# A two-layer graph network on one core: ten rounds of gathers placed between the set-up's tables, and the blocks' pieces dealt out singly

## The chip, the core and the metric

The kernel runs on one core of a Trainium2 chip. The engines named below are PE (matrix multiply; its weight loads are shown apart as PEld), DVE (vector), ACT (scalar), POOL, and SP, which here only issues transfers. The metric is the device time of one execution in microseconds (us), the median of the runs. Lower is better.

## The reference

Two rounds of mean aggregation over 200,000 directed edges between 12,500 nodes of 256 features, a third matrix product, a residual and a layer norm:

```python
def _sage_conv(x, src, dst, W_l, b_l, W_r):
    msgs = x[src]
    agg = jax.ops.segment_sum(msgs, dst, num_segments=N_NODES)
    deg = jax.ops.segment_sum(jnp.ones((src.shape[0],), x.dtype), dst, num_segments=N_NODES)
    mean = agg / jnp.maximum(deg, 1.0)[:, None]
    return mean @ W_l + b_l + x @ W_r
h = jax.nn.relu(_sage_conv(x, src, dst, W1_l, b1, W1_r))
h = jax.nn.relu(_sage_conv(h, src, dst, W2_l, b2, W2_r))
out = layernorm(x + (h @ W3 + b3))
```

Edges come sorted by `dst`, and `dst` is drawn as the square of a uniform number: nodes with a low number have many edges, the others few.

## The kernel before

**Blocks, hot and cold.** The 12,500 nodes are 98 blocks of 128 rows (`NB`). The first ten blocks in layer 1 (fourteen in layer 2) are hot. They are handled as a dense product: `count` builds a matrix of how often each source occurs for 256 targets, `product` (L605 to L614) multiplies it with all of `x`, held as three bf16 parts that add up to float32. The parts of `x` are made by `split_rows` (98 calls, each: load a block into `x_sb`, two casts on ACT and two subtractions on DVE in `exact`, store of `parts`); those of `h` are made in `first_block`.

**Rounds.** The edges of cold blocks go in rounds. A round is four gathers of 128 rows each from DRAM into one of four buffers `got` (L532, POOL), a 0/1 table `one` (L466, DVE), and four matmuls into `part_ps` (L543, PE). When a group of edges is complete (one or two rounds) `part_ps` is copied to `some` (L549, ACT), a round later `summed` multiplies it with a second 0/1 table `two` (L555; L560 for the in-degrees) and DVE adds the product to a ring of sums (`sums` L567, `degs` L563). Layer 1 has 269 rounds, that is 1,076 gathers; layer 2 has 247 rounds and 988 gathers. Layer 2 gathers rows of `h_d`, which layer 1 has just written, so its first gather waits for the last store of layer 1.

**Blocks in pieces.** When a block's sums are complete, its rows run through the weights: `first_block` in three pieces, `last_block` in five, each piece ending in a `yield`. `first_block`'s second piece multiplies the degree row with a one (L860) into column `ps[:, NC, 0:1]` of a PSUM tile, DVE reads it there (`deg`, L862, then the reciprocal L863), and then PE transposes the block's rows `x_sb` into the same tile (L814), which ACT copies to `own_t` (L816). `sage` (L837, L839, DVE L842 and L843, ACT L845) makes the layer's rows.

**What sets the order.** PE and POOL run in the order in which the program is written (`manual_schedule`), so a wait of one PE instruction holds up all behind it. The order on DVE, ACT and SP is chosen by a planner at build time, and each of them then also works strictly through its own list. `layer` writes the order of each layer: per round first `gathered(i)`; then half of the pieces that are due, where a quarter of all pieces of the up to three open blocks (`MOST`) counts as due; half of the dense work that is due (`fill`, by a table of costs); then `summed` of the round before; then the other half of pieces and of dense work. The first open block always goes first.

**Buffers that matter here.** `x_sb` is one pool of three buffers, used by `split_rows` and by the blocks alike (L803 to L811). `exact` has one buffer `rest` (L587), also used by both. `own` has one buffer.

**Set-up.** Before the layers, a set-up turns the edge lists into tables (L175 to L402): transposes on PE, many small operations on DVE. Its SBUF is given up at its end, and the two matrices `counts` (cleared by ACT at L430) lie in that space. PE and POOL follow the planner's order in the set-up, and the manual order only begins with `layer`.

Of the kernel before, what the change touches and what calls it, by code (L numbers as in the profile page):

```python
# [47 lines left out]
def by_runs(  # L48
# [123 lines left out]

    with tc.tile_pool(name="setup", bufs=1) as su, \
# [140 lines left out]


# [19 lines left out]
        for g, (c0, c1) in enumerate(spans):  # L335
            n = c1 - c0
            for begins, to, name in ((start, key_t[g], "key"), (nxt_first, after_t[g], "aft")):
# [12 lines left out]
            nc.vector.tensor_copy(offs[g], off_f[:, lows[g]:highs[g]])  # L350


# [7 lines left out]
                                       op1=OP.mult, accum_out=test())  # L360
        scr2 = su.tile([P, len(groups)], F32, name="scr2")
# [73 lines left out]
    part_pool = ctx.enter_context(tc.tile_pool(name="part_ps", bufs=1, space=PSUM))  # L435
    sum_pool = ctx.enter_context(tc.tile_pool(name="sum_ps", bufs=1, space=PSUM))
# [4 lines left out]
    REGS = 8  # L441

    class Values:


        def __init__(self, row, i0, engine, top):
            self.row, self.i0, self.engine, self.top, self.have = row, i0, engine, top, {}

        def at(self, i):
            if i not in self.have:  # L450
                a = i - self.i0
                n = min(REGS, self.row.shape[1] - a)
                _, v = nc.values_load_multi_w_load_instructions(
                    self.row[0:1, a:a + n], engines=[self.engine], min_val=0, max_val=self.top,
                    skip_runtime_bounds_check_because="it is clamped where it is made")
                self.have = {i + k: v[k] for k in range(n)}
            return self.have[i]


    def select(g, r, second):  # L460

        t0, n = groups[g]
        lo, c0 = (lo_t2, C2) if second and t0 // P == C2 else (lo_t, C0)
        a = t0 - c0 * P + r
        one = chosen_pool.tile([P, G, W], F32, name="one", bufs=AHEAD + 1)
        nc.vector.tensor_tensor(  # L466
            one, lo[:, a:a + n * (G - 1) + 1:n].unsqueeze(2).to_broadcast([P, G, W]),
            lane_b[:, :W].unsqueeze(1).to_broadcast([P, G, W]), op=OP.is_equal)
        if r < n - 1:
            return one, None  # L470
        two = chosen_pool.tile([P, P], F32, name="two", bufs=AHEAD + 2)
        nc.vector.tensor_scalar(two, lane_b, lo2[:, g:g + 1], None, op0=OP.is_equal)
        return one, two

    def left_after(g):

        return NB if g == len(groups) - 1 else min(max(int(at_least(groups[g + 1][0]) // P), 0), NB)

    AHEAD = 2

    MOST = 3

    def layer(table, hot, block, n_pieces, dense, dense_cost):
# [3 lines left out]

        def advance(i):
            b, p, left = queue[i]
            next(p)  # L490
            queue[i] = b, p, left - 1
            if left == 1:
                done.add(b)
                del queue[i]
                return True

        def begin():
            while waiting and len(queue) < MOST:
                b, *of = waiting.pop(0)
                queue.append((b, block(b, *of), n_pieces))  # L500
                advance(len(queue) - 1)

        def pieces(n):

            i = 0
            for _ in range(min(n, len(queue))):
                if not advance(i):
                    i += 1
            begin()
# [12 lines left out]
        begun = hot // P  # L522
        at = Values(place, 0, DVE, RN - 1)
        chosen = {i: select(*rounds[i], second) for i in range(AHEAD)}

        def gathered(i):

            (gr, r), g = rounds[i], got[i % NGOT]
# [764 lines left out]
```

## Time and profile before

| | |
|---|---|
| time, three runs | 2920.19, 2927.65, 2936.41 us; median 2927.65 us |
| the profiled execution | 3466.66 us, its span 3464.9 us |
| mean granted PE clock in it | 0.868 |
| PE busy in the span | 2583.9 us (75%), 18,630 matmuls |
| POOL busy | 2029.7 us (59%), nearly all gathers |
| DVE busy | 1468.1 us (42%) |
| ACT busy | 1250.0 us (36%) |
| DMA | 676.45 MB, mean 195 GB/s |

The profiled execution took 18% longer than the median of the runs. Sums over the profile are therefore made against 3464.9 us first and carried over to 2927.65 us in a second step. A group's row gives line, engine, operation, output and inputs, count, then busy time in us and the mean of one in ns, then the idle time of the engine just before these instructions and what ended it. A row of waits gives the engine and line that waited, what it waited for, the total in us, the number of times and the longest. In a timeline each row begins with the start and the duration in us, and ends in brackets with the idle time before it and what ended that.

The stages lie so in the span: set-up up to 74 us, layer 1 up to 1888 us, layer 2 behind it, last gather at 3404 us.

### The profile page before, as it was taken

The numbers are of one execution on the slowest core, as the hardware profiler recorded it, in microseconds if no ns is written. First come the engines' busy times: TensorE is split into PE (matmuls) and PEld (weight loads), VectorE is DVE, ScalarE is ACT, GpSimd is POOL, SyncE is SP. The second block draws the span as 40 slices with busy tenths as digits, with TensorE's granted clock in tenths as the row PEclk, the third lists the DMA queues.
The fourth block names the chain that finished last, engine by engine and source line by source line (L and its number), as shares of the span: only waits on it lengthen the run. The fifth ranks groups of instructions, "written<-read, shape, count | busy, mean of one in ns | idle before, by whom it ended". The sixth has DMA issues, their size and how long they took to land.

```text
span 3464.9 us, 54167 instructions
## 1 busy us (share of the span) xinstructions
PE 2583.9 (75%) x18630; PEld 1705.5 (49%) x18630; DVE 1468.1 (42%) x4350; ACT 1250.0 (36%) x2702; POOL 2029.7 (59%) x2074
## 2 busy tenths in 40 slices
PE   2544658778878878888886677777878887878885
PEld 1121225545545556656654354444555555656664
DVE  7656655444444444445453023333223233333433
ACT  1323655455554555556553013333111111111222
POOL 3554656665665565666663666666666666566661
PEclk9666679879979989989998888888889899999998
DMA  4544577648648648656753565666777787766762
GB/s 89 153 147 147 183 210 229 195 128 279 202 144 269 202 144 263 207 159 194 222 162 111 184 204 184 187 186 192 243 240 246 243 258 240 230 211 215 223 213 69
DMA packets 408134, 676.45 MB, mean 195 GB/s; under 512 B 59659, under 2 KB 266537, under 8 KB 407849
## 3 DMA queue, kind: packets, MB, share of 16 engines
q1 hardware_dynamic: 303415, 400.51, 36.8%
q0 software_dynamic: 99072, 270.66, 25.8%
q10 hardware_dynamic: 5362, 1.72, 0.3%
q8 instruction: 149, 2.44, 0.3%
q14 instruction: 136, 1.11, 0.1%
HBM read 582.80 MB, written 89.87 MB: 194 GB/s over the span
## 4 chain that ended last, share of the span: by engine, by line
PE 60%; issue 8%; another core or an unknown queue 8%; DVE 4%; DMA 3%; ACT 3%; SPq 0%; POOL 0%; ACTq 0%; DVEq 0%
PE dense_ps L614 22%; PE part_ps L543 8%; PE block_ps L837 6%; PE count_ps L682 6%; PE block_ps L839 5%; PE sum_ps L555 4%; PE block_ps L814 3%; PE block_ps L895 3%; ACT counts L688 1%; PE sum_ps L560 1%; DMA rows<-x_d 1%; DMA rows<-h_d 1%; PE count_ps L686 1%; DVE pick L637 1%
## 5 line engine op out<-in xcount | busy, mean ns | idle before, releaser
L532 POOL DMA_INDIRECT got<-in_x_dram,src_t x1076 | 1083.2, 1007 | 764.9 <-PE part_ps L543 282.7
L532 POOL DMA_INDIRECT got<-h_d,src_t x988 | 944.4, 956 | 610.1 <-issue 247.9
L614 PE MATMUL dense_ps<-counts,rows 128*128 128x256 bf16 x7056 | 1025.9, 289 | 84.3 <-issue 49.3
L688 ACT CAST counts<-count_ps 128x392 f32 (+2 forms) x1052 | 716.1, 681 | 633.2 <-PE count_ps L686 145.9
L614 PEld LDWEIGHTS <-rows 128*128 128x128 bf16 x7056 | 702.3, 103 | 338.0 <-issue 142.4
L543 PE MATMUL part_ps<-got,one 128*32 128x257 f32 (+1 forms) x4128 | 384.9, 438 | 96.2 <-issue 47.1
L682 PE MATMUL count_ps<-pick,low 128*128 128x392 bf16 (+2 forms) x1052 | 371.1, 381 | 104.8 <-DVE pick L637 33.3
L637 DVE TENSOR_SCALAR pick<-steps,key_t 128x686 bf16<-128x686 f16 (+2 forms) x748 | 300.0, 411 | 254.1 <-PE count_ps L682 77.3
L466 DVE TENSOR_TENSOR one<-lo_t,lane_b 128x128 f32<-128x128 bf16 x516 | 148.0, 287 | 539.6 <-PE part_ps L543 143.6
L549 ACT COPY some<-part_ps 128x257 f32<-128x257 f32 (+1 forms) x361 | 136.8, 379 | 562.0 <-remote 215.5
L567 DVE TENSOR_TENSOR sums<-sums,sum_ps 128x256 f32 x361 | 148.3, 411 | 303.2 <-remote 119.7
L555 PE MATMUL sum_ps<-two,some 128*128 128x128 f32 x1444 | 246.6, 297 | 5.4 <-remote 2.8
L555 PEld LDWEIGHTS sum_ps<-two,some 128*128 128x128 f32 x1444 | 212.6, 208 | 23.5 <-issue 8.5
L543 PEld LDWEIGHTS part_ps<-got,one 128*32 128x32 f32 x4128 | 89.9, 114 | 245.9 <-issue 178.0
L814 PE MATMUL block_ps<-ident,x_sb 128*128 128x128 f32 x196 | 50.7, 348 | 207.2 <-DVE deg L862 96.7
L842 DVE TENSOR_TENSOR own<-block_ps,biases 128x256 f32<-128x256 f32 x196 | 83.0, 423 | 259.8 <-PE block_ps L839 123.2
L682 PEld LDWEIGHTS <-low 128*128 128x128 bf16 x1052 | 108.3, 106 | 155.7 <-issue 72.1
L816 ACT COPY own_t<-block_ps 128x256 f32<-128x256 f32 x294 | 109.1, 374 | 188.7 <-PE block_ps L814 76.0
L563 DVE TENSOR_TENSOR degs<-degs,sum_ps 1x128 f32 x186 | 51.0, 274 | 232.0 <-PE part_ps L543 67.7
L895 PE MATMUL block_ps<-w_sb,own_t 128*128 128x256 f32 x392 | 122.1, 440 | 36.4 <-ACT own_t L816 25.3
L837 PE MATMUL block_ps<-w2l_sb,sums 128*128 128x256 f32 x336 | 112.6, 464 | 46.3 <-DVE sums L567 18.8
L641 DVE TENSOR_TENSOR low<-low_t,lane_b 128x512 bf16<-128x512 bf16 x187 | 128.1, 685 | 43.1 <-PE count_ps L686 28.1
(177 smaller groups left out, 2672.1 us busy)
## 6 DMA issues: line engine op xcount, KB each, us to landing
rows<-h_d SPq DMA_DIRECT2D x343, 384.0 KB
rows<-x_d SPq DMA_DIRECT2D x245, 384.0 KB
x_sb<-in_x_dram SPq DMA_DIRECT2D x291, 128.0 KB
count_d<-counts SPq DMA_DIRECT2D x28, 896.0 KB
counts<-count_d SPq DMA_DIRECT2D x28, 896.0 KB
x_d<-parts SPq DMA_DIRECT2D x98, 192.0 KB
h_d<-parts SPq DMA_DIRECT2D x98, 192.0 KB
got<-in_x_dram,src_t POOLq DMA_INDIRECT x1076
```

The lines of the kernel that those rows point to most:

```text
L532: nc.gpsimd.indirect_dma_start(out=g[:, j, :D], out_offset=None, in_=table, in_offset=bass.IndirectOffsetOnAxis(ap=src_t[:, e:e + 1], axis=0))
L543: nc.tensor.matmul(part_ps[j * W:(j + 1) * W, :width], lhsT=one[:, j], rhs=g[:, j, :width], start=r == 0, stop=r == n - 1)
L555: nc.tensor.matmul(sum_ps[:, c], lhsT=some[:, c * P:(c + 1) * P], rhs=two, start=True, stop=True)
L567: nc.vector.tensor_add(own, own, sum_ps[:, :NC])
L614: nc.tensor.matmul(ps[:, c], lhsT=rows[:, b % 2, k, c * P:(c + 1) * P], rhs=c_sb[:, b, :DN], start=False, stop=b == NB - 1 and k == 2 and ...
L637: nc.vector.tensor_scalar(r[:, :w * NB], steps[:, :w * NB], key_t[g][:, t - lo_g:t - lo_g + 1], None, op0=OP.is_equal)
L682: nc.tensor.matmul(ps[:, :(b - a) * NB], lhsT=s, rhs=r[:, a * NB:b * NB], start=True, stop=alone)
L688: nc.scalar.copy(to[:, :, bass.ds(n0 + a, b - a)], ps[:, :(b - a) * NB].rearrange("p (d s) -> p s d", s=NB))
L814: nc.tensor.transpose(ps[:, c], t[:, c * P:(c + 1) * P], ident)
L837: nc.tensor.matmul(ps[:, 0], lhsT=agg[:, c], rhs=wl[:, c], start=c == 0, stop=c == NC - 1)
L839: nc.tensor.matmul(ps[:, 1], lhsT=own_t[:, c], rhs=wr[:, c], start=c == 0, stop=c == NC - 1)
L895: nc.tensor.matmul(y[:, 0], lhsT=h2_t[:, c], rhs=w3_sb[:, c], start=c == 0, stop=c == NC - 1)
```

## The change

It has two parts. **Rounds in the set-up:** the state of the rounds moves into a class `Gathers` with a method `step`, which writes one round and returns the group that is ready to be summed. The first ten rounds of layer 1, with their matmuls and sums, are written into the set-up: one ahead of the tables for the hot blocks, one behind each of the seven pairs of tables, and two later. The manual order of PE and POOL begins there, so the set-up's remaining transposes stand in it too. `layer` starts at round ten. **Pieces:** each round has three turns. A turn advances one block by one piece at most, a block no sooner than two turns after its last piece (`APART`), and at most two blocks are open (`MOST`). Each turn is followed by a third of the dense work, and `summed` stands ahead of the third turn. With it, buffers and waits change: `split_rows` has its own buffers (`split_sb`, two), the blocks' `x_sb` has two, `exact` writes the rest over its input (or over `own`) and not into `rest`; the degree is copied by ACT together with the transposed rows and read by DVE from SBUF; `last_block` loads `x_sb` in its third piece instead of its first and adds the bias in the fourth instead of the third.

```diff
+    class Gathers:
+        def __init__(self, table, second):
...
+            self.chosen = {i: select(*self.rounds[i], second) for i in range(AHEAD)}
+            self.i, self.last = 0, None
+
+        def step(self):
+            before = self.last
+            self.last = self.gathered(self.i) if self.i < len(self.rounds) else None
+            self.i += 1
+            return before
...
         nc.vector.memset(zeros_b, 0.0)
+        ctx.enter_context(tc.manual_schedule(engines={PE, POOL}))
+        gathers_1 = Gathers(x, False)
+
+        def early_round():
+            before = gathers_1.step()
+            if before:
+                gathers_1.summed(*before, set())
+
+        early_round()
...
             nc.vector.tensor_copy(offs[g], off_f[:, lows[g]:highs[g]])
-
+            early_round()
+
+        early_round()
 
         nxt_f = su.tile([P, CH, P], F32, name="nxt_f")
...
         nc.vector.scalar_tensor_tensor(scr[:, C0:], rel[:, C0:], float(W), nxt_f[:, C0:], op0=OP.is_ge,
                                        op1=OP.mult, accum_out=test())
+        early_round()
...
-    MOST = 3
+    MOST, APART = 2, 2
...
         def begin():
-            while waiting and len(queue) < MOST:
+            if waiting and len(queue) < MOST:
                 b, *of = waiting.pop(0)
-                queue.append((b, block(b, *of), n_pieces))
-                advance(len(queue) - 1)
+                p = block(b, *of)
+                next(p)
+                queue.append([b, p, n_pieces - 1, turn + APART])
-        def pieces(n):
-            i = 0
-            for _ in range(min(n, len(queue))):
-                if not advance(i):
-                    i += 1
+        def pieces():
+            nonlocal turn
+            turn += 1
+            q = next((q for q in queue if q[3] <= turn), None)
+            if q:
+                next(q[1])
+                q[2:] = q[2] - 1, turn + APART
+                if q[2] == 0:
+                    done.add(q[0])
+                    queue.remove(q)
             begin()
...
-            n = -(-sum(left for _, _, left in queue) // 4)
-            pieces(-(-n // 2))
-            due = dense_cost * min(1.0, (i + 1) / (len(rounds) - 8))
-            fill(spent + (due - spent) * 0.5)
...
-            pieces(n // 2)
-            fill(due)
+            before = gathers.step()
+            due = dense_cost * min(1.0, (i + 1 - i0) / (n - i0 - 8))
+            for part in range(3):
+                if part == 2 and before:
+                    gathers.summed(*before, done)
+                    while begun < left_after(before[0]):
+                        waiting.append((begun,))
+                        begun += 1
+                pieces()
+                fill(spent + (due - spent) / (3 - part))
...
-    def exact(t, s):
-        rest = work.tile([P, D], F32, name="rest", bufs=1)
+    def exact(t, s, rest):
...
     def split_rows(b):
-        t = load_rows(x, N, b, "x_sb")
+        t = load_rows(x, N, b, "split_sb")
         s = work.tile([P, 3, D], BF16, name="parts")
-        exact(t, s)
+        exact(t, s, t)
...
-        t = work.tile([P, D], F32, name=name, bufs=MOST if table is x else 2)
+        t = work.tile([P, D], F32, name=name)
...
-    def transposed(t, ps, name):
+    def transposed(t, ps, name, more=0):
...
-        s = work.tile([P, NC, P], F32, name=name)
-        nc.scalar.copy(s, ps[:, :NC])
-        return s
+        s = work.tile([P, NC * P + 1], F32, name=name)
+        n = NC * P + more
+        nc.scalar.copy(s[:, :n], ps.rearrange("p c l -> p (c l)")[:, :n])
+        return s[:, :NC * P].rearrange("p (c l) -> p c l", l=P), s[:, NC * P:]
...
             nc.tensor.matmul(ps[:, NC, 0:1], lhsT=deg_row, rhs=ones[0:1, 0:1], start=True, stop=True)
-            deg = work.tile([P, 1], F32, name="deg")
-            nc.vector.tensor_scalar(deg, ps[:, NC, 0:1], 1.0, None, op0=OP.max)
+        x_t, deg = transposed(x_sb, ps, "own_t", int(of_ring))
+        if of_ring:
+            nc.vector.tensor_scalar(deg, deg, 1.0, None, op0=OP.max)
             nc.vector.reciprocal(rdeg[:, b:b + 1], deg)
-        x_t = transposed(x_sb, ps, "own_t")
         yield True
...
-        exact(h, s)
+        exact(h, s, own)
...
         h_sb = load_rows(h_d, NB * P, b, "h_sb")
-        x_sb = load_rows(x, N, b, "x_sb")
...
         if of_ring:
             nc.scalar.copy(agg, zeros)
+        x_sb = load_rows(x, N, b, "x_sb")
+        yield True
+        h2_t, _ = transposed(h2, turned(), "own_t")
         nc.vector.tensor_add(x_sb, x_sb, biases[:, 2])
-        yield True
-        h2_t = transposed(h2, turned(), "own_t")
         yield True
...
-    with tc.manual_schedule(engines={PE, POOL}):
-        layer(x, HG1 * DN, first_block, 3, staged(stages_1), cost_of(stages_1))
-        layer(h_d, HG * DN, last_block, 5, staged(stages_2), cost_of(stages_2))
+    layer(gathers_1, first_block, 3, staged(stages_1), cost_of(stages_1))
+    layer(Gathers(h_d, True), last_block, 5, staged(stages_2), cost_of(stages_2))
```

## The prediction

> **What bounds the kernel now.** I read the totals first, then the chain that ended last, then the waits of PE and POOL, then the same by stages, and last the timeline where the waits are longest. From the page, the chain and the gathers:
>
> ```profile
> PE 60%; issue 8%; another core or an unknown queue 8%; DVE 4%; DMA 3%; ACT 3%; SPq 0%; POOL 0%; ACTq 0%; DVEq 0%
> ...
> L532 POOL DMA_INDIRECT got<-in_x_dram,src_t x1076 | 1083.2, 1007 | 764.9 <-PE part_ps L543 282.7
> L532 POOL DMA_INDIRECT got<-h_d,src_t x988 | 944.4, 956 | 610.1 <-issue 247.9
> ```
>
> The chain is PE's: POOL has no share. The second thing to see is how near POOL is all the same. Between two gathers POOL always loses some 0.31 us ("issue": 508.5 us in 1,652 waits, next fence), so a gather costs 1.007 + 0.308 us in layer 1 and 0.956 + 0.308 in layer 2: 1,076 x 1.315 + 988 x 1.264 = 2,664 us. With the 27 us before the first gather, 38 us between the layers and 60 us after the last gather, POOL alone needs **2,789 us**, 139 less than the median of 2927.65. The profiled execution is 537 us longer than the median, and the chain gives 8% to "issue" and 8% to an unknown queue, together about as much. My reading: much of those two is the recording's own, and without it PE is quicker and POOL sets the pace wherever it isn't stopped. The profile can't prove that.
>
> The waits of PE, then of POOL:
>
> ```profile
> PE block_ps L814 <- DVE deg L862: 96.7, 70, 3.9
> PE block_ps L814 <- DMA x_sb<-in_x_dram: 78.0, 7, 15.2
> PE block_ps L814 <- ACT h L845: 58.9, 31, 5.5
> ...
> PE block_ps L895 <- ACT own_t L816: 25.3, 17, 4.6
> ...
> PE block_ps L814 <- DVE rest L594: 19.4, 2, 17.9
> ```
> ```profile
> POOL got L532 <- issue: 508.5, 1652, 1.1
> POOL got L532 <- PE part_ps L543: 371.1, 133, 24.7
> ```
>
> Four of PE's waits belong to the blocks' pieces and one to the split. Two kinds must be kept apart: waits of about 1 to 2 us (deg, h, own_t), which POOL rides out with four buffers, and waits of 15 us, in which POOL stops too. The stages show where (start:end, length, then busy us of PE, PEld, DVE, ACT, POOL, granted clock, DMA share, GB/s):
>
> ```profile
> 27.00:75.00 48.00, 14.20 (x54) 8.46 (x54) 44.44 (x162) 2.90 (x4) 19.26 (x16) 1.00 0.21 61
> 75.00:97.00 22.00, 6.43 (x28) 1.51 (x28) 10.84 (x30) 21.78 (x4) 8.26 (x8) 0.71 0.20 54
> 97.00:200.00 103.00, 61.69 (x300) 21.97 (x297) 75.50 (x210) 22.14 (x59) 64.88 (x63) 0.70 0.55 167
> 200.00:400.00 200.00, 95.27 (x513) 42.66 (x511) 126.46 (x329) 79.39 (x182) 107.23 (x105) 0.67 0.51 156
> 800.00:1000.00 200.00, 163.18 (x1281) 111.67 (x1278) 87.14 (x253) 109.82 (x222) 122.35 (x126) 0.89 0.69 214
> ```
>
> From 97 to 400 neither PE nor POOL is full. In the timeline of layer 1, one such stop and the end of the set-up:
>
> ```profile
> 218.75 0.66 PE L814 MATMUL block_ps<-ident,x_sb 128*128 128x128 f32 x2 [14.63 <-DMA x_sb<-in_x_dram]
> 222.53 0.95 POOL L532 DMA_INDIRECT got<-in_x_dram,src_t  x1 [10.37 <-PE part_ps L543]
> ```
> ```profile
> 74.20 22.01 ACT L430 COPY counts<-zero 128x13034 f32<-128x13034 f32 x2 [44.22 <-DVE scr L400]
> 75.78 1.34 POOL L532 DMA_INDIRECT got<-in_x_dram,src_t  x1 [24.73 <-PE part_ps L543]
> ```
>
> While PE waited, DVE and ACT did nothing but split rows: the block's load had its turn in the shared `x_sb` pool behind some six splits at 2.4 us each.
>
> **The change, part by part**, in us of the profiled execution.
>
> *Rounds in the set-up.* POOL stood 24.7 us for the set-up's end (row above) and 12.1 us more up to 98.3, because `some` was queued on ACT behind the 22 us of clearing. Ten rounds are 40 gathers. Beside the busy DVE of the set-up the first 16 took 19.22 us, 1.20 each, so 40 x (1.20 + 0.30) = 60: the last ends at 87, its strip is multiplied about 1.9 later (after the fourth gather of layer 2, which ended at 1893.35, the strip began at 1895.23). [...] The row decides: 1.20 in the set-up against 0.95 at 1888 to 1913 with DVE idle, the worst one 2.52; so I pay 0.25 each, no more.
> The order costs something. On PE the tables of pair g now stand behind strip g, at 27.2 + 6.0(g+1) + 1.9: the last pair goes at 71 and not at 58. DVE's own additions are ten `one` at 0.287 and four or five sets of `two`, `degs`, `sums` (0.97): 7 us. Its tests (59.2 to 74.0, 15 us) either fill the waits or follow. The set-up ends at 81 to 88; take 85, so clearing ends at 107, 11 later. By then POOL has issued 40 and four more rounds, 56 gathers, against 31 at that time now: 25 x 1.31 = 33 ahead. The count work starts 11 later, and DVE, 73% busy from 97 to 200, has to make it up. **-25**; between -37 (both stops gone, no price) and +11 (the delay alone).
>
> *Own buffers for the split and for blocks.* PE's 78.0 + 19.4 = 97.4; POOL's part_ps waits between 98.3 and 600 sum to 98.8. The new load waits only for a block two before. What is late next is POOL: between 97 and 500 it has 229 gathers at 1.037 + 0.308 = 308 of 403 us, so at most 95; DVE, with about 260, is close behind. **-90**, between -95 and -50 (the splits' stores and `parts`, still two buffers shared with blocks, could hold a block). `rest` and `own`, in place: nothing, hidden by the two turns to the same block's next piece; uncovered, a chain of five operations of 0.4 us per block.
>
> *The degree through ACT.* 70 waits, 96.7 us, go: nothing on DVE stands any more between L860 and the transposes. What replaces it is one column more in a copy of 0.37 us, and L862 and L863 with two turns before L843 needs them. L860's own wait for `degs` stays (31.6). PE alone waits here, 45 of them from 600 to 1600 where PE is 82% busy and POOL 61%. **-48** if PE paces, 0 if POOL does; -97 at best.
>
> *Singly dealt pieces.* Counting turns by the code, a block of layer 2 now waits half a round between two of its pieces (the first open block is often taken in both halves); two turns are two thirds of a round, 4 us at 6.2 us a round, against a chain L842, L843, L845 of 0.42 + 0.48 + 0.42 and its queues. Of 58.9 + 25.3 = 84 I take half. The later `x_sb` load in layer 2 has two turns, 4 us, for a landing of 2.7 (issued 3402.65, read at 3405.35) and for whatever SP waits for ahead of it: price +10. **-32** if PE paces, 0 if POOL does; bounds -84 and +80. Two open blocks are enough: layer 2's last blocks come at half a block a round, 2 of 3 turns. By the same count one block less is open behind the last round: **-3**.
>
> *The clock.* [...] 0.67 to 0.70 against 0.89, eight matmuls of a strip 1.08 against 0.64; [...] PE doesn't end that stage, so I count nothing.
>
> **The forecast, POOL's pace.** Then only the stops of POOL come back: -25 - 90 - 3 = -118, and 2927.65 - 118 = **2,810**, 21 above POOL's own 2,789. These stops (24.7 + 12.1 + 98.8 = 136) are also just what separates the median from 2,789, which is my reason for this case. Chance 0.42, own range 2,785 to 2,850.
>
> **Rivals.** (1) *PE's pace*, as the chain of the profile says: -25 - 90 - 48 - 32 - 3 = -198 of 3464.9, 5.7%, so 2,760. For it: the chain; against it: POOL's sum, unless a gather is quicker unrecorded. 0.22. (2) *The block waits all the same*, now for `parts` or for SP: half of the 90 and of the 25 goes, 2,870. For it: SP's and ACT's strict lists; against: the loads come a round early. 0.16. (3) *Slower: DVE stopped in front of the bias.* L889 stands in DVE's list, and its load in SP's behind loads of `rows`, which wait 3.1 us on average for PE to free a buffer in layer 2 (322.0 us in 105 waits) and 10.9 at worst. While DVE waits, `one`, `sums` and picks wait, then PE, then POOL. 98 blocks x 2 us = 196, less 118: 3,005; it decides from 1.2 us a block. For it: L889 waits 28.7 us now; against: it has a piece's matmuls and 4 us ahead of it. 0.13. (4) *No difference*: the stops belong to the recording. Against: 15 us is six splits, not a hiccup. 0.07.
>
> A change within 0.5% (2,913 to 2,942) can't be told from none. Faster 0.42 + 0.22 + 0.16 = 0.80, same 0.07, slower 0.13. The range goes from 2,715 (PE's pace with both costs nearer their best) to 2,930.
>
> **What would show it.** Right: no wait of PE for `x_sb` or `rest` beyond a few us; L862 gone from PE's waits; some 40 gathers issued by 90 us; DVE and POOL fuller from 97 to 400, clock above 0.8. Wrong: clearing of `counts` starting after 95; L889 waiting more than 100 us in all; deg's wait gone and the time down by 150 or more (rival 1).

## The result and the profile after

The changed kernel takes **2906.97 us** (median of 6 runs, 2895.08 to 2912.04) and the kernel before 2935.14 us (6 runs) beside it: ratio **0.9909**, 95% interval 0.9882 to 0.9935. The forecast was 118 us less than before; 28 us came.

The profiled execution of the kernel before that the prediction was made from (3466.66 us) is like those of one chip among the five used later, where this kernel takes 3472.27 us (median of 11 runs). On the other four it takes about 2,930, as in the runs above. So ratios are only formed with runs of the kernel before on the same chip, and below "before" is a new recording on a chip of the common kind (label b1_before_again, span 2936.8 us).

From the page of the changed kernel: the engines' busy time, the chain that ended last, and the two groups of gathers (busy us, mean ns, then the idle time ahead of them).

```profile
PE 2394.6 (82%) x18630; PEld 1632.6 (56%) x18630; DVE 1471.2 (51%) x4350; ACT 1253.6 (43%) x2702; POOL 2065.3 (71%) x2074
...
PE 54%; DMA 19%; POOL 8%; issue 7%; DVE 6%; ACT 4%; DVEq 0%; SPq 0%; ACTq 0%; POOLq 0%
...
L243 POOL DMA_INDIRECT got<-in_x_dram,src_t x1076 | 1116.7, 1038 | 446.5 <-issue 274.2
L243 POOL DMA_INDIRECT got<-h_d,src_t x988 | 946.4, 958 | 343.1 <-issue 285.3
```

The work is the same, PE still has the largest share of the chain, and a gather of layer 1 has become dearer (1.038 us; 1.010 in the new recording of before). The unknown queue is gone from the chain, as it is in b1 (whose chain accounts for 85% of its span): only the recordings of the slower chip show it.

The change's path shows best in where POOL stands. The table gives the start in us of the n-th gather, counted in the timelines of five kernels (columns 4 to 6 are experiments of the next section; the chips differ, but on each the kernel before takes about 2,930 us).

| gather | before | changed | parts apart (b4) | split spread (e3) | no split (d4) |
|---|---|---|---|---|---|
| 56 | 140.5 | 108.8 | 109.0 | 108.5 | 105.5 |
| 240 | 430.2 | 370.6 | 378.7 | 376.3 | 358.1 |
| 280 | 497.3 | 441.5 | 433.0 | 431.4 | 413.3 |
| 400 | 654.5 | 641.2 | 607.2 | 597.7 | 573.2 |
| 1076, last of layer 1 | 1567.8 | 1564.9 | 1523.6 | 1512.5 | 1488.3 |
| 2064, last of layer 2 | 2882.2 | 2854.6 | 2818.7 | 2793.0 | 2773.0 |

The changed kernel is 32 us ahead at gather 56, as forecast, and 60 at gather 240. Then it loses 46 of these in the next 160 gathers, and at the end of layer 1 it leads by 3. The 25 us that are left of the gain come from layer 2.

Two things eat the lead. Call it a stop when POOL idles for more than 0.5 us between two gathers, and count of it what goes beyond the usual 0.31. Then from gather 56 to the end of layer 1 the changed kernel has 95 us of stops and the kernel before 89, and its gathers are busy for 1,049 us and not 1,026. So of the 29 us of lead that go, 23 go in longer gathers and 6 in stops. The stops were to become fewer and only moved: between gathers 56 and 240 they fell from 41 to 5 us, between 240 and 400 they rose from 13 to 55.

What stops POOL is seen in the waits of PE and of POOL from 100 to 640 us (line that waited, releaser: total, times, longest). Before:

```profile
PE block_ps L814 <- DMA x_sb<-in_x_dram: 58.1, 6, 16.2
PE count_ps L682 <- DVE pick L637: 29.2, 20, 12.0
PE block_ps L814 <- DVE rest L594: 18.0, 1, 18.0
...
POOL got L532 <- PE part_ps L543: 57.0, 16, 11.5
```

The changed kernel, same stretch:

```profile
PE block_ps L886 <- DVE own L869: 54.3, 7, 19.1
PE count_ps L706 <- DVE pick L661: 23.8, 20, 3.7
...
POOL got L243 <- PE part_ps L254: 57.5, 16, 17.9
```

The wait for `x_sb` is gone, and so is the one for `rest`. In their place stands a wait that did not exist: the product of the degree row (L886) waits for a PSUM buffer that DVE's L869 is late to read. For POOL the sum has not changed: 57.0 us in 16 waits, 57.5 in 16. The timeline of the changed kernel at the longest stop (start, duration, in brackets the idle time before and its end) shows who is late:

```profile
456.15 0.40 ACT L617 CAST parts<-split_sb 128x256 bf16<-128x256 f32 x1 [6.15 <-DMA split_sb<-in_x_dram]
...
456.58 0.43 DVE L618 TENSOR_TENSOR split_sb<-split_sb,parts 128x256 f32<-128x256 f32 x1 [5.91 <-ACT parts L617]
...
457.93 1.61 SPq L626 DMA_DIRECT2D x_d<-parts  x1
458.27 0.42 DVE L868 TENSOR_TENSOR own<-block_ps,biases 128x256 f32<-128x256 f32 x1
...
460.08 0.44 SPq L833 DMA_DIRECT2D split_sb<-in_x_dram  x1
...
462.59 0.40 ACT L617 CAST parts<-split_sb 128x256 bf16<-128x256 f32 x1 [4.80 <-DMA x_d<-parts]
463.02 0.43 DVE L618 TENSOR_TENSOR split_sb<-split_sb,parts 128x256 f32<-128x256 f32 x1 [4.32 <-ACT parts L617]
...
464.13 0.48 DVE L869 SCALAR_TENSOR_TENSOR own<-block_ps,rdeg,own 128x256 f32<-128x256 f32 x1
...
464.66 0.58 PE L886 MATMUL block_ps<-ones,degs 1*128 1x1 f32 x2 [19.08 <-DVE own L869]
...
470.80 0.95 POOL L243 DMA_INDIRECT got<-in_x_dram,src_t  x1 [17.91 <-PE part_ps L254]
```

Read it from the bottom. POOL waited for PE, PE for L869, and L869 stood in DVE's strict list between subtractions of the split (L618). These waited for ACT's casts (L617), and the casts for two DMAs in turn: the load of `split_sb`, and the store of `parts`, whose two buffers the split still shares with the blocks. In this stop the block's instruction was only queued behind rows of the split that had not arrived or found no buffer. Over all seven waits of L886, 54.3 us, DVE stood idle for 24 us in front of operations of the split; in the rest it mostly worked through its list.

### The profile page after: what moved, and what is told of

Same layout as the page of the kernel before. It is cut to its first block, busy times and chain, and to the rows that moved or that the text cites. A ratio compares the mean times of both kernels' runs of the same rounds, so it can differ in the third digit from the quotient of the medians.

```text
span 2908.8 us, 54100 instructions
## 1 busy us (share of the span) xinstructions
PE 2394.6 (82%) x18630; PEld 1632.6 (56%) x18630; DVE 1471.2 (51%) x4350; ACT 1253.6 (43%) x2702; POOL 2065.3 (71%) x2074
## 4 chain that ended last, share of the span: by engine, by line
PE 54%; DMA 19%; POOL 8%; issue 7%; DVE 6%; ACT 4%; DVEq 0%; SPq 0%; ACTq 0%; POOLq 0%
PE dense_ps L638 19%; POOL got L243 8%; PE part_ps L254 7%; PE block_ps L863 6%; DMA got<-h_d,src_t 5%; PE count_ps L706 5%; PE block_ps L865 5%; PE sum_ps L265 4%; DMA x_sb<-in_x_dram 3%; DMA rows<-h_d 3%; DMA rows<-x_d 3%; PE block_ps L839 2%; PE block_ps L921 2%; DMA split_sb<-in_x_dram 2%; PE sum_ps L270 2%
## 5 line engine op out<-in xcount | busy, mean ns | idle before, releaser
L243 POOL DMA_INDIRECT got<-in_x_dram,src_t x1076 | 1116.7, 1038 | 446.5 <-issue 274.2
L638 PE MATMUL dense_ps<-counts,rows 128*128 128x256 bf16 x7056 | 976.9, 279 | 51.3 <-DMA rows<-h_d 27.7
L638 PEld LDWEIGHTS <-rows 128*128 128x128 bf16 x7056 | 671.3, 100 | 287.5 <-issue 88.6
L254 PE MATMUL part_ps<-got,one 128*32 128x257 f32 (+1 forms) x4128 | 359.7, 422 | 192.1 <-DMA got<-h_d,src_t 123.0
L706 PE MATMUL count_ps<-pick,low 128*128 128x392 bf16 (+2 forms) x1052 | 343.4, 354 | 57.0 <-ACT counts L712 27.0
L259 ACT COPY some<-part_ps 128x257 f32<-128x257 f32 (+1 forms) x361 | 136.1, 377 | 431.4 <-PE part_ps L254 428.2
L868 DVE TENSOR_TENSOR own<-block_ps,biases 128x256 f32<-128x256 f32 x196 | 83.0, 423 | 230.9 <-PE block_ps L865 230.2
L706 PEld LDWEIGHTS <-low 128*128 128x128 bf16 x1052 | 101.8, 100 | 152.3 <-DVE pick L661 54.2
L842 ACT COPY own_t<-block_ps 128x256 f32<-128x256 f32 (+1 forms) x294 | 110.0, 375 | 123.7 <-PE block_ps L839 121.2
L871 ACT ACTIVATE h<-own 128x256 f32<-128x256 f32 x196 | 81.4, 415 | 179.3 <-DVE own L869 179.2
L710 PE MATMUL count_ps<-aft,low 128*128 128x98 bf16 x614 | 131.9, 215 | 0.0
L863 PE MATMUL block_ps<-w1l_sb,sums 128*128 128x256 f32 x352 | 113.9, 452 | 2.1 <-DVE sums L277 1.8
L863 PE MATMUL block_ps<-w2l_sb,sums 128*128 128x256 f32 x336 | 104.1, 437 | 11.3 <-DVE sums L277 11.1
```

The lines of the kernel that those rows point to most:

```text
L243: nc.gpsimd.indirect_dma_start(out=g[:, j, :D], out_offset=None, in_=self.table, in_offset=bass.IndirectOffsetOnAxis(ap=src_t[:, e:e + 1], ...
L254: nc.tensor.matmul(part_ps[j * W:(j + 1) * W, :width], lhsT=one[:, j], rhs=g[:, j, :width], start=r == 0, stop=r == n - 1)
L259: nc.scalar.copy(some[:, :width], part_ps[:, :width])
L638: nc.tensor.matmul(ps[:, c], lhsT=rows[:, b % 2, k, c * P:(c + 1) * P], rhs=c_sb[:, b, :DN], start=False, stop=b == NB - 1 and k == 2 and ...
L706: nc.tensor.matmul(ps[:, :(b - a) * NB], lhsT=s, rhs=r[:, a * NB:b * NB], start=True, stop=alone)
L863: nc.tensor.matmul(ps[:, 0], lhsT=agg[:, c], rhs=wl[:, c], start=c == 0, stop=c == NC - 1)
```

## The experiments

All variants below are of one of the two kernels, most with a few lines changed. Ratios are to the kernel before on the same chip, with the 95% interval.

| label | what it is | ratio | interval |
|---|---|---|---|
| b1_before_again | before | 1.0017 | 0.9993 to 1.0042 |
| b2_rounds_alone | before, with the ten rounds | 1.0029 | 1.0014 to 1.0045 |
| b3_pieces_alone | changed, without the ten rounds | 0.9942 | 0.9917 to 0.9967 |
| b4_parts_apart | changed, the split's parts in own buffers | 0.9784 | 0.9759 to 0.9809 |
| d1_after_again | changed | 0.99 | 0.9871 to 0.9929 |
| d2_parts_and_loads | b4 with three load buffers for the split | 0.9786 | 0.9755 to 0.9817 |
| d3_old_dealing_in_layer_2 | changed, old dealing in layer 2 | 0.9983 | 0.9968 to 0.9998 |
| d4_after_no_split | changed, without the split | 0.9679 | 0.9641 to 0.9716 |
| e1_pieces_and_parts_apart | b4 without the ten rounds | 0.9782 | 0.9763 to 0.9801 |
| e2_split_without_subtractions | d2, DVE's part of the split left out | 0.9675 | 0.9652 to 0.9697 |
| e3_split_spread | d2, split planned at 1.2 | 0.972 | 0.9705 to 0.9735 |
| f1_spread_without_rounds | e3 without the ten rounds | 0.976 | 0.9736 to 0.9784 |
| f2_spread_alone | changed, split planned at 1.2 | 0.9848 | 0.9826 to 0.9871 |
| f3_spread_more | d2, split planned at 1.6 | 0.9764 | 0.9739 to 0.9789 |

The four of label c ran on the chip on which the kernel before takes 3472.27 us, and stand apart further down.

**The two halves of the change, each alone.** b1 is the kernel before as it stands; b2 has the class `Gathers` and the early rounds but the old pieces and buffers; b3 has all but the early rounds, whose ten calls are left out, so that `layer` begins at round 0:

```
-        early_round()
```

> The kernel before, recorded a second time. Theory A (the first recording was itself slow: everything waited on something unknown for 8% of the span): the span comes out near 2,930, a gather still costs 1.25 to 1.34 us of POOL, and POOL's stops behind part_ps from 97 to 600 us are well below the 98.8 of the first recording, about 60 or less. Theory B (the stops of 15 us are the kernel's own, as the prediction had it): they are there again, near 95 us, also in a span of 2,930.

> Only the first part of the change: ten rounds in the set-up; pieces, buffers and waits as before. If the rounds are worth what POOL gets ahead by (25 in the prediction's sum, 33 at most): 2,900 to 2,910 against 2,935. If the later clearing of counts takes it back: within 5 us of before. If they account for the whole measured gain: ratio 0.991.

> Only the second part: pieces dealt singly, own buffers, degree through ACT; no rounds in the set-up. Prediction's theory: the stops in the split stage go, 2,845 or below (-90). Theory of replacement (a block now stops for the split on DVE's list, 52.6 us of PE waits for own L869 in the changed kernel): between -20 and +5 us against before.

b1 takes 2938.79 us, b2 2938.97, b3 2912.53, beside a before of 2933.14. So the rounds alone bring nothing, and the pieces with their buffers 0.6%. b1's span of 2936.8 us and POOL's 57.0 us are what its theory A expected. The set-up's price is in the rows of ACT's clearing of `counts`, which begins when the set-up's space is free (min/median/max ns, then the first and last start in us); in b1 and in the changed kernel:

```profile
L430 ACT COPY counts<-zero x2: 11047/11050/11054, 74.6 to 85.5; 128x13034 f32<-128x13034 f32 x2
```
```profile
L550 ACT COPY counts<-zero x2: 11048/11050/11053, 94.9 to 105.9; 128x13034 f32<-128x13034 f32 x2
```

The set-up ends 20 us later. POOL has 32 us of gathers more behind it, but the count work and what follows on DVE begin 20 us later, and from 95 to 440 us DVE is busy for 263 of 345 us. b1's recording also shows that the degree's wait was small on this kind of chip, and that the prediction's 96.7 us in 70 waits belonged to the other:

```profile
PE block_ps L814 <- DVE deg L862: 22.4, 80, 1.2
```

**The shared `parts`.** The edit takes the split's results out of the blocks' pool (and, for space, puts them and the loads into buffers that layer 2 uses later):

```
     def split_rows(b):
-        t = load_rows(x, N, b, "split_sb")
-        s = work.tile([P, 3, D], BF16, name="parts")
+        t = load_rows(x, N, b, "z")
+        s = work.tile([P, 3, D], BF16, name="split_parts", tag="h_sb")
```

> The changed kernel with the split's parts in two buffers of their own, not shared with the blocks' parts. If the stops of PE for own L869 (52.6 us, six of 5 to 19 us, from 97 to 500) come from the shared parts buffers: they fall below 15 us and the time to about 2,870 (POOL stood 39 us behind part_ps there). If they come from DVE's order of work alone: they stay above 35 us and the time stays at 2,900 to 2,912.

2865.95 us, 41 less than the changed kernel's 2906.97, which was not run beside it (by the two ratios it is 37). d2 is the same with three load buffers (`load_rows(x, N, b, "z", 3)`), d1 is the changed kernel again on d2's chip.

> The changed kernel itself, so that the other three runs here have it on their own chip. Both theories: 0.988 to 0.994 of the kernel before on a chip where that takes 2,93x us, and lower, about 0.97, on one where it takes 3,47x.

> The changed kernel with the split's parts in buffers of its own and three load buffers for the split. If the shared parts buffer alone held the split back: the same as with the parts alone, 0.975 to 0.981 of the kernel before, and 41 us under the changed kernel. If the loads held it back as well: another 5 to 15 us less, and the stops of GpSimd between gathers 240 and 400 go from 12 us to nearly none. If the split is held by the order of VectorE's list (its casts behind the blocks' sums) whatever the buffers: no gain over the parts alone, and the last store of the split stays at about 508 us.

d1 takes 2899.87 us, d2 2871.81, before 2931.76. The parts are worth 28 us here, side by side; a third load buffer adds nothing to b4's ratio. Two more pairs of the table part them as well: b3 and e1, without the ten rounds (0.9942 to 0.9782, some 47 us), and f2 and e3, with the split planned at 1.2 (0.9848 to 0.972, some 38 us, a third load buffer with it). In d2 PE's and POOL's waits from 100 to 640 us are these:

```profile
PE count_ps L706 <- DVE pick L661: 35.6, 26, 9.9
PE count_ps L691 <- DVE pick L661: 23.0, 25, 2.0
...
POOL got L243 <- PE part_ps L254: 18.8, 14, 6.6
```

L886 is no longer among the longest, and POOL's waits for PE's strips are down from 57.5 to 18.8 us. In all four pairs POOL's stops between gathers 240 and 400 fall, from 46 to 55 us to 7 to 12, and the time by 28 to 47 us; so that the shared `parts` cost this is shown. By which way is not. The engines have the same instructions, but not in the same order: in b4 the planner gave some 760 of DVE's 4,350 another place. In the changed kernel subtractions of the split stand between L868 and L869 in four blocks before 640 us, in b4 in none; but in e3, with 7 us of stops, they stand there in six, so this place alone doesn't make the stops. And ACT still waits for the split's loads, 82.2 us in 45 waits from 100 to 640 us in b4 and 77.1 in 35 in the changed kernel; only its waits for stores of `parts`, 21.0 us in 10, are gone in b4. How much comes from the buffers themselves and how much from the list that the planner made with them stays open.

**What the split costs in all.** d4, and three kernels of label c, split only the first block and store that one 98 times:

```
+        if b == 0:
+            t = load_rows(x, N, b, "z")
+            exact(t, split_once, t)
+        nc.sync.dma_start(x3_d[:, b], split_once)
```

97 loads, 194 casts and 194 subtractions are left out, so the dense products of layer 1 read other rows; the 98 stores stay (the expectation of d4 names them as left out, which they are not). c4 is the changed kernel with three load buffers for the split and its parts still shared.

> The kernel before without the work of the split: one block is split, and its parts are stored 98 times (97 loads, 194 casts and 194 subtractions are left out, so layer 1's hot blocks are computed from the wrong rows). Theory S (the split's chain of load, cast, subtract, cast, subtract, store sets the pace up to 460 us): POOL's stops from 100 to 500 us, 54 us in the second recording, go, and the time falls by 45 to 60 us, to about 2,880. Theory P (POOL or DVE sets that stage anyway): it falls by less than 20.

> The pieces alone, no rounds in the set-up, without the work of the split (as in the run before; layer 1's hot blocks from the wrong rows). Theory S: the stops of 50 us from 400 to 500 us go, 2,912 becomes 2,850 to 2,862. Theory P: above 2,895.

> The changed kernel without the work of the split (same part left out). Theory S: the stops of 61 us from 200 to 560 us go, and the ten rounds then keep their lead of 30 us to the end: 2,815 to 2,830, so some 30 us under the pieces alone without the split, against 6 us with it. Theory P: above 2,890, and no more than 10 us under the pieces alone.

> The changed kernel with three buffers instead of two for the split's loads (parts still shared with the blocks). If the loads are what makes the split's chain longer than before (ACT waits 77.8 us for them in the changed kernel): the last store of the split moves from 539 to about 480 us and the time to 2,875 or below. If the shared parts are: last store at 520 or later, time within 10 us of 2,907.

> The changed kernel without the split of x in layer 1 (97 loads, 194 casts, 194 subtractions and 97 stores of it are left out, so layer 1's dense products read rows that were not made). If the split's chain ate the lead of the ten rounds: 50 to 70 us under the changed kernel and GpSimd's stops between gathers 240 and 400 under 10 us, and not more than 25 us under the version with parts and loads apart. If the lead is lost whatever happens to the split (PE's pace): within 20 us of the changed kernel.

On the chip where the kernel before takes 3472.27 us: before without the split 3406.13 (0.9809, 0.9769 to 0.9848), b3 without it 3371.6 (0.9718, 0.968 to 0.9756), the changed kernel without it 3348.67 (0.9646, 0.9608 to 0.9684), and c4 3401.4 (0.9809, 0.9776 to 0.9842). There the ten rounds are worth 3371.6 - 3348.67 = 23 us, close to the predicted 25; this pair differs from the others in the chip as well as in the split. In c4 POOL's stops between gathers 240 and 400 sum to 68 us with a longest of 25; c3 has 33 us there, none longer than 2.5. So a third load buffer without own parts leaves long stops. How much it helps is not shown: the changed kernel as it stands was not run on that chip. On the ordinary chip d4 takes 2832.89, 67 us less than the changed kernel: the split costs that much, 28 of it, on this chip, through the shared parts.

**The other 39 us of the split** (d2 against d4). e2 leaves out DVE's 194 subtractions and keeps both casts; what is stored is the first cast three times, so layer 1's dense products read other numbers here too. e3, f2 and f3 change one number of the plan, the cost that it reckons for splitting a block (1.6 in f3):

```
-        exact(t, s, t)
-        nc.sync.dma_start(x3_d[:, b], s)
+        nc.scalar.copy(s[:, 0], t)
+        nc.scalar.copy(s[:, 1], t)
+        nc.sync.dma_start(x3_d[:, b], s[:, 0:1].to_broadcast([P, 3, D]))
...
-    COST_DENSE, COST_DEGREES, COST_SPLIT = 0.7, 1.6, 0.8
+    COST_DENSE, COST_DEGREES, COST_SPLIT = 0.7, 1.6, 1.2
```

> Parts and loads apart, and the split without VectorE's part: its 194 subtractions are left out (both casts of ScalarE stay, the first cast is stored three times, so layer 1's dense products read other numbers). If the 39 us that still lie between this version and the one without any split come from VectorE's work beside the gathers: gathers 40 to 240 fall from 1.09 to 1.15 us to 1.04 to 1.06 and the time by 15 to 30 us, ratio 0.968 to 0.974. If they come from loads, casts and stores (queues, ScalarE): the gathers stay at 1.09 and more, and the time within 8 us of 0.978.

e2 takes 2838.13 us beside a before of 2930.48: nearly all of the 39 us are won. Part of it is the gathers. One row for the gathers and the matmuls that read them, from 110 to 370 us, busy us of PE, PEld, DVE and POOL with the counts; d2, then e2:

```profile
110.00:370.00 260.00, 39.39 (x352) 8.69 (x352) 0.00 (x0) 200.08 (x178) 0.72 0.65 195
```
```profile
110.00:370.00 260.00, 42.29 (x392) 9.35 (x392) 0.00 (x0) 195.00 (x189) 0.76 0.68 201
```

A gather took 200.08 / 178 = 1.124 us beside the whole split and 195.00 / 189 = 1.032 us without the subtractions: 0.092 less. Over the same 200 gathers, 81 to 280, it is 1.122 against 1.049, some 15 us. The counts say it more plainly: 11 gathers more in the same 260 us.

The limit of this experiment: without DVE in its chain the split also ran earlier, its stores from 28.3 to 279.5 us and not from 117.3 to 469.2, so the first dense product came at 405.1 us and not at 436.4. How the rest of the 39 us divides between the two is not shown.

> Parts and loads apart, and the split planned at a cost of 1.2 instead of 0.8 per block, so that its stage is stretched over more gathers. If the split runs behind its plan and stops PE and with it the gathers: the last stops between gathers 240 and 400 go (12 us now), 5 to 15 us faster than 0.978. If the plan of the stages behind it is the tighter one, PE's list ends later and nothing is won, or up to 10 us lost.

> The changed kernel with one number changed: the split planned at 1.2 instead of 0.8 per block; its parts stay shared with the blocks. If the shared parts hold the split whatever its plan: no more than 10 us off the changed kernel, 0.987 to 0.991, stops of 40 us and more between gathers 240 and 400. If the split was only planned too densely: as much as with parts and loads apart, 0.971 to 0.976.

> Parts and loads apart, the split planned at 1.6. If the split still crowds VectorE at 1.2: another 5 to 10 us, 0.968 to 0.970. If stretching it only moves the dense work behind it into a tighter plan: slower than at 1.2 by 0 to 15 us.

e3 takes 2848.66 us, and is the **fastest kernel here that leaves nothing out**: 0.972, 82 us under the kernel before. f2 (2890.15 beside 2932.28) lies between the two theories: 0.5% better than the changed kernel, and its stops between gathers 240 and 400 are still 46 us, so spreading helps but the shared parts hold it. f3 (2868.42) is back at d2's ratio. What e3 gained was not expected in this form: between gathers 240 and 400 its stops are 7 us against 11, and of the 25.5 us by which its last gather starts earlier than d2's (2793.0 against 2818.5) 11 lie in layer 1 and 15 in layer 2, whose part of the program was not touched. From first to last gather layer 2 took 1,246 to 1,263 us in the twelve recordings with the new dealing, so more than half of e3's lead over d2 is not explained by the split. In the recordings most of it lies in POOL's stops of layer 2, 2 us in e3 and 14 in d2; but two recordings of the changed kernel differ there as well (10 and 2). DVE and ACT have the same order in layer 2 in both kernels; why the stops differ stays open.

**Rounds, once the split is out of the way.** e1 is b4 without the ten rounds, f1 is e3 without them.

> Pieces singly, with buffers of their own, and the split's parts apart, without the ten rounds in the set-up. With the rounds this stood at 0.978 of the kernel before. If the rounds' lead is kept once the split doesn't wait for the blocks' stores: 20 to 30 us slower than with the rounds, ratio 0.985 to 0.989. If the lead is lost whatever the split does: the same as with the rounds, 0.977 to 0.980.

> Pieces singly, parts and loads apart, the split planned at 1.2, without the ten rounds in the set-up. With the rounds it stood at 0.972 of the kernel before. If the rounds are worth nothing whatever the split does (PE has its own work behind them): 0.971 to 0.974. If the split's place in the plan was what ate their lead: 20 to 30 us slower than with them, 0.979 to 0.983.

e1 takes 2869.1 us, 0.9782 against b4's 0.9784 and d2's 0.9786: the rounds are worth nothing here. The first expectation was wrong. f1 takes 2867.22 beside 2932.28, 0.976 against e3's 0.972: 12 us, with intervals that just don't meet. The recordings show the lead of 31 us at gather 56 and 29 at gather 280 in d2 over e1, and 22 at gather 600, 9 at gather 1000. From gather 56 to the end of layer 1, 23 us of it go: 16 in longer gathers (busy for 1,051 us in d2, 1,035 in e1) and 7 in longer stops. The other pairs fit this: in f1 and e3 the gathers of layer 1 take 6 us more with the rounds, which are worth 12, and in c2 and c3 no more, and they are worth 23. Each is one recording, and two of the same kernel differ by 5 us. Why later gathers are longer when rounds were put early is not shown; nor is it tested whether PE, busy for 327 of 360 us from 640 to 1000 in d2, lengthens the stops.

**Layer 2.** d3 deals the pieces of layer 2 as before (three open blocks, several pieces at once) and keeps all the rest, the later load of `x_sb` too:

```
-    layer(Gathers(h_d, True), last_block, 5, staged(stages_2), cost_of(stages_2))
+    layer_old(Gathers(h_d, True), last_block, 5, staged(stages_2), cost_of(stages_2))
```

> The changed kernel with layer 2's pieces dealt as in the kernel before (three blocks at once, several pieces in a turn), layer 1 unchanged. If the gain that was kept (25 of 28 us lay in layer 2, where GpSimd's stops went from 35 to 10 us) comes from single pieces: 20 to 28 us slower than the changed kernel, no difference from the kernel before left. If it comes from the later load of the block's x rows, which is kept here: no slower than 5 us over the changed kernel.

2925.82 us, 26 more than d1. Two of POOL's waits from 1600 to 2860 us in d1, where 0.3 us each is the usual pause, and the two longest in d3 apart from "issue":

```profile
POOL got L243 <- PE dense_ps L638: 8.5, 28, 0.3
POOL got L243 <- PE part_ps L254: 7.8, 20, 1.8
```
```profile
POOL got L243 <- PE block_ps L893: 22.8, 21, 4.5
POOL got L243 <- PE part_ps L254: 22.0, 28, 3.1
```

With the old dealing several pieces of blocks stand between two strips, and POOL waits for them up to 4.5 us; dealt singly, they leave it 2 us of stops in d1, against 30 in d3. Of d1's gain of 32 us this is 26: nearly the whole gain of the change.

## Why the prediction was wrong

The direction was right, and the end lies in the range, but of 118 us 28 came, and the direction was luck: of the three terms that made up the 118 (-25, -90, -3) the changed kernel shows at most 6 to 10 us, and 26 of the 28 us come from the pieces in layer 2, which the forecast had put at 0.

- **What bounds the kernel.** That POOL's pace sets the end wherever POOL isn't stopped was a good guide: the last gathers in the table stand in the order of the times. The sum of 2,789 us is not contradicted: the kernel without the split, the fastest, comes to 2832.89. Wrong was the reading that much of the profiled execution's 537 us were "the recording's own". b1 was recorded the same way and took 2936.8 us in its span; the long one is what another chip takes without a recording too. The sentence "The profile can't prove that" was the place to stop and to take the sums as sums of an unlike run. Besides, the 118 us, read from a span of 3464.9, were taken off 2927.65 as they stood; carried over like rival 1's sum they would have been 100.
- **Own buffers for the split and for blocks, -90: the step that failed**, in both its parts. The size came from the other chip: 98.8 us of POOL's stops there, 57.0 in b1. And "what is late next is POOL" was false: next was the split's own chain, through DVE's list, with 54.3 us in 7 waits where 58.1 in 6 had been, and POOL's waits for PE stayed at 57 us, so that of the 90 nothing came. The bound named in brackets, that `parts`, "still two buffers shared with blocks, could hold a block", was the right mechanism, taken as an end of the range and not as the likeliest case. In the stop shown it works by a longer way than thought: the block doesn't wait for `parts` itself, but for DVE, which waits for ACT, which waits for a store of `parts` or a load of the split. With own parts (b4) the wait for stores goes, that for loads stays, and the planner puts the split elsewhere in DVE's list.
- **Rounds in the set-up, -25.** The start came as worked out: 33 us ahead were forecast at gather 56, 31.7 were measured. The fortieth gather was forecast to end at 87 and ended at 82.7. These forty took 1.141 us each on average, 2.90 at most; 1.20 had been reckoned. The set-up's end came 20 us later and not 11, at the very edge of the sign that was set (after 95). The forecast of what remains was wrong: it was kept only without the split on the other chip (23 us); 12 came with the split spread, none with the parts apart, and in the changed kernel 6 to 10, with intervals that overlap (b3's 0.9942 against 0.9909). The term put at nothing is the length of the gathers behind the set-up: the 0.25 us were paid for 40 gathers, but all gathers of layer 1 together took 29 us longer than in b1, 23 of these after the 56th (10 of the 23 in b3 too, without the rounds).
- **The degree through ACT, 0 by POOL's pace**: its wait is gone from PE's list, and it was 22.4 us in 80 short waits on this kind of chip. It wasn't tried alone.
- **Singly dealt pieces, 0 by POOL's pace, -32 by PE's**: measured 26 us (d3 against d1). It was put at 0 since POOL was thought to ride out short waits; in layer 2 POOL's stops, of 4.6 us at most, sum to 35 us in b1, 30 in d3, and 10 and 2 in the two recordings of the changed kernel.
- **Tail, -3**: 54.6 us from the last gather's start to the span's end before, 54.2 after. Nothing.
- **Clock**: "above 0.8" from 97 to 400 was wrong: there it is 0.70 in the changed kernel. From 95 to 240 and from 240 to 440 us it is 0.70 and 0.71, and 0.71 in both in b1, with PE busy for 222.9 of these 345 us against 212.5 in b1. What sets the granted clock in this stretch is not shown.
- **Rivals.** PE's pace (2,760) was not it. "The block waits all the same" was the nearest in mechanism; in size "no difference" was (2,913 to 2,942, against 2,870 for rival 2 and 2,906.97 measured). Rival 3's wait is larger than its sign of 100 us, but the sign says nothing: on this kind of chip it was as large before. The changed kernel, then b1:

```profile
L917 DVE TENSOR_TENSOR x_sb<-x_sb,biases x98: 393/426/483, 1588.0 to 2889.0; 128x256 f32<-128x256 f32 x98
...
  DMA x_sb<-in_x_dram: 119.0, 69
```
```profile
DVE x_sb L889 <- DMA x_sb<-in_x_dram: 122.5, 69, 6.7
```

The 28.7 us that the prediction gave for it came from the other chip (30.8 in the whole of that recording).

With b1's numbers in place of the other chip's, the same sum would have been -25 - 57 - 3 = -85, or 2,850 from 2,935. The changed kernel doesn't reach that; e3, with the split's parts apart and its plan stretched, does (2848.66), though in part by layer 2.

## What to carry to other kernels

When two users of a pool are parted, follow every buffer that they share, to the last store: one that is left shared (here `parts`) can give the old wait back under another name, and a list that is worked through in strict order can carry it to work that doesn't use that buffer. Look at the new order too: an edit of buffers alone also changed the planner's lists. A profiled execution that is far from the median of the runs can be another situation, not the same one with an overhead, and then ratios of its waits to its span don't carry over (here POOL's waits for strips from 100 to 640 us: 98.8 of 3,464.9 us in the first recording, 57.0 of 2,936.8 in b1). And a lead that an early start gives is not yet a gain: ask what the early work delays (here the set-up's end, by 20 us) and whether each later step still costs the same (with the rounds the gathers behind the set-up took 16 us longer, d2 against e1).

## What the runs showed of the hardware

The same kernel takes about 2,930 us on four chips and 3,472 us on a fifth. A gather is as long there (1.007 and 0.956 us in the two layers of the first recording, 1.010 and 0.957 in b1), the granted TensorE clock is 0.868 and not 0.918, PE is busy for 2583.9 us and not 2396.0, and the chain that ended last holds 8% of waits for an unknown queue (9% in c1), which the chains of the other chips don't show, as far as they reach back. Both layers lose: from the first to the last gather layer 1 takes 1,823 us and layer 2 1,516 in the first recording, 1,540 and 1,281 in b1; POOL's stops in layer 2 are 270 us against 35. From the page of c1, its chain:

```profile
PE 65%; issue 10%; another core or an unknown queue 9%; DVE 7%; ACT 4%; DMA 4%; SPq 0%; ACTq 0%; DVEq 0%; POOL 0%
```

What this queue was isn't shown by the recordings.

In three stretches a gather took longer on POOL the busier DVE was beside it: 0.958 us in the changed kernel's layer 2 (DVE busy for 390 of 1,000 us from 1700 to 2700), 1.124 beside the split in d2 (213 of 260 us from 110 to 370), 1.032 there in e2, without the split's subtractions (185 of 260). By what way is not shown. The 36 gathers from 25 to 60, around the end of the set-up, took 1.27 and 1.28 on average in the two recordings of the changed kernel; without the early rounds the gathers of these numbers took 1.04 in b1, 1.06 in b3 and 1.03 in e1, but 1.21 in f1. On the average of such stretches the tax is a third at most (1.28 against 0.958; single gathers took up to 3.67 us in the changed kernel), and that over all of layer 1 it is 1.038 against 1.010 costs the changed kernel 29 us of POOL's time.
